# Three of four blocks of turned rows change partition halves by GpSimd's DMA queue instead of narrow TensorE matmuls

## The chip, the cores and the metric

The kernel runs on one core of one Trainium2 chip. The core has TensorE (PE in the profile; PEld is its weight load), VectorE (DVE), ScalarE (ACT), GpSimd (POOL) and SyncE (SP), each with its own instruction queue; they meet at semaphores. DMAs are issued from SP's, ACT's or POOL's queue and are carried by the core's 16 DMA engines. The metric is device time in microseconds, the median of several executions.

## What is computed

The program is a graph network of four layers on N = 3327 nodes with 64 features and one dense adjacency matrix. Each layer is `x = layernorm(x + f(x, adj))`. Layer 0 is cheap here, because its residual needs no product with the adjacency matrix that survives the normalisation in this kernel. The change lies in layer 1, a hyperbolic attention layer, cut to its core:

```python
x_tan = _logmap0(x, C)
left  = x_tan @ att_W[:D] + att_b
right = x_tan @ att_W[D:]
adj_att = jax.nn.sigmoid(left + right.T) * adj
x_local = _logmap(x[:, None, :], x[None, :, :], C)      # for every pair of nodes
support_t = jnp.einsum('ij,ijd->id', adj_att, x_local)
return _proj(_expmap(x, support_t, C), C)
```

For every pair (i, j) a product of two rows gives an angle; the sigmoid of a sum gives an attention weight, which is multiplied by the adjacency entry; and the weighted rows are summed over j. Layers 2 and 3 multiply the adjacency matrix (or counts of its nonzero entries) with the features.

## The kernel before

The nodes are padded to 3328, in 26 blocks of 128. The 64 features take half of the 128 partitions, so two blocks are stacked: a tile of 128 partitions holds block b (0 to 12) in the upper 64 partitions and block b + 13 in the lower 64. The tiles are `ri` and `lj`, rows of i and of j with nodes on partitions, and `riT` and `ljT`, the same turned, with features on partitions.

`near_sphere` (line 1302) is layer 1 for the data at hand. Its main loop runs over `tiles`: for two column ranges of i, for each of the 26 blocks of j, for two chunks of 416 columns. `products` (line 1391) multiplies a block of `ljT` with a chunk of `riT` on TensorE, once in each half of the partitions, into `pq`. `angle` (1406) applies the arc tangent on ScalarE. `attention` (1362) makes the weights: a sigmoid on ScalarE (`sigmoid`) and a product with the adjacency tile on GpSimd (`times`); it is a generator, and its caller decides how far it goes. `gather` (1413) combines angle and weight on VectorE, and `collect` (1436) sums over j on TensorE into `acc`.

A block of j must be multiplied with the i of both halves, so it is needed in both halves of the partitions. `ljT[0]` holds the blocks where the stacking put them, `ljT[1]` holds them with the halves changed. There are two ways to make `ljT[1]`. `wrong` (1487) does it on TensorE: for each block and half a matmul with the identity, 64 columns wide, into the other half of a PSUM tile, which an engine then copies out. `change_over` (1497) does it by two DMAs from `ljT[0]` to `ljT[1]`, one for each half. Before the change, columns of blocks 9 to 12 (with 22 to 25) are made by `wrong` and all others by `change_over` on SP's queue.

The order of the instructions of TensorE, ScalarE, VectorE and GpSimd is written out by hand at lines 1542 to 1657 (`manual_schedule`): each engine's queue follows the order of these lines. `alone` and `bank` (1532 to 1540) take a PSUM tile, run a turn on TensorE at once, and return a function that copies the result out when it is called: on ScalarE by default, on VectorE where `copy` is given. The blocks of j are visited in the order 25, 24, 23, 22, 12, 11, ..., so the first product needs block 12's columns of `ljT[1]`, the third (`products(2)`) block 11's.

The steps around the change, in order: `scaled` and `rows_of_i` on VectorE finish `lj` and `ri`; `after` (1567), a copy of one column by GpSimd, holds that engine's queue until VectorE has finished the last of them; `spread_a` and `spread_b` copy the left terms; `next(start)` runs the first sigmoid and the first `times`; then follow the turns `rows_j` (`right`, blocks 9 to 12), `spread_c`, `spread_d`, `rows_a` (`turn`, blocks 0 to 3), `changed` (`wrong`, blocks 9 to 12) and `rows_b` (`turn`, blocks 4 to 7), each with its copy. A second `next(start)`, the small turns of `prep_few`, the turns of `prep_fours`, and the first products come after these. The blocks of the adjacency matrix are loaded by SP: `kept` (four whole blocks, line 144) and `at` (line 1347).

GpSimd's queue is used for DMAs elsewhere too: at the end of layer 2 it writes and reads back rows of counts (`t_rows`, lines 432 and 464).

Of the kernel before, what the change touches and what calls it, by code (L numbers as in the profile page):

```python
# [23 lines left out]
D = 64  # L24
# [5 lines left out]
def slot(jb):  # L30

    return 2 * (jb % NBH) + jb // NBH
# [50 lines left out]
def kernel(  # L83
# [11 lines left out]
    nc = tc.nc  # L95
# [16 lines left out]
    lj = const.tile([P, NB, D], F32, name="lj")  # L112
# [1077 lines left out]
    with tc.tile_pool(name="l1", bufs=1) as l1:  # L1190
# [18 lines left out]
        with tc.tile_pool(name="l1a", bufs=1) as l1a, tc.tile_pool(  # L1209
# [30 lines left out]
            for i, g in enumerate(range(0, NBH, 4)):  # L1240
                n = min(4, NBH - g)
# [25 lines left out]
            for i, (g, n) in enumerate(turned):  # L1267
                if i == 3:
                    nc.tensor.matmul(n_low, lows, ones, start=True, stop=True)
                for k in range(g, g + n):  # L1270
                    nc.tensor.matmul(
                        pr[:, k].rearrange("p h t -> p (h t)"), xT[:, k * P : (k + 1) * P],
                        attw_c, start=True, stop=True,
# [28 lines left out]
        def near_sphere(mT, ljT_0, xm, sq_e, t_e):  # L1302
# [3 lines left out]
            with tc.tile_pool(name="n1", bufs=1, reuse_waits="tile") as n1, tc.tile_pool(  # L1306
# [10 lines left out]
                ljT = [ljT_0, n1.tile([P, HALF], F32, name="ljT_1")]  # L1317
# [44 lines left out]
                def attention(pair):  # L1362

                    if pair >= len(tiles) // 2:
                        return
                    cp, jb, _ = tiles[2 * pair]
                    at, sl = ats[pair], slot(jb)
                    sg = n1w.tile([P, 2, 2 * CW], F32, tag="sg", bufs=4, name=f"sg_{pair}")
                    lbs = lbh[:, :, cp * 2 * CW : (cp + 1) * 2 * CW]
                    sgs[pair] = sg  # L1370

                    def sigmoid(of):
                        nc.scalar.activation(  # L1373
                            sg[:, :, of], lbs[:, :, of], AF.Sigmoid, bias=rb[:, sl : sl + 1]
                        )

                    def times(h, of):
                        nc.gpsimd.tensor_tensor(  # L1378
                            sg[:, h, of], sg[:, h, of], at[:, h, of], ALU.mult
                        )  # L1380

                    chunks = (slice(0, CW), slice(CW, 2 * CW))
                    sigmoid(slice(0, 2 * CW) if pair else chunks[0])
                    times(slice(0, 2), chunks[0])
                    yield
                    if not pair:
                        sigmoid(chunks[1])
                    times(0, chunks[1])
                    yield
# [104 lines left out]
                            )  # L1494
                    return ljT[1][:, b * P : (b + n) * P], pt[:, : n * P]

                def change_over(b, n):
                    of = slice(b * P, (b + n) * P)
                    nc.sync.dma_start(ljT[1][D:, of], ljT[0][:D, of])
                    nc.sync.dma_start(ljT[1][:D, of], ljT[0][D:, of])  # L1500

                def turn(pt, b, n):

# [7 lines left out]
                def made(pt, make, b, n, at_once=True):  # L1511
                    dst, src = make(pt, b, n)

                    def copy(to=nc.scalar.copy):
                        to(dst, src)
                        if make is right and b < 9:
                            if at_once:
                                change_over(b, n)
                            else:
                                changes.append((b, n))  # L1520

                    return copy
# [9 lines left out]
                def bank(which, make, b, n):  # L1532

                    pt = n1c.tile([P, 4 * P], F32, tag=f"acc{which}", name=f"prep_{make.__name__}_{b}")
                    return made(pt, make, b, n)

                def alone(make, b, n):

                    pt = n1p.tile([P, 4 * P], F32, name=f"first_{make.__name__}_{b}")
                    return made(pt, make, b, n)  # L1540

                with tc.manual_schedule(
# [21 lines left out]
                    scaled(0, 5)  # L1564

                    after = n1.tile([P, 1], F32, name="after")
                    nc.gpsimd.tensor_copy(after, lj[:, 0, :1])
                    spread_a, spread_b = bank(0, left, 0, 4), bank(1, left, 13, 4)
                    spread_a()
                    spread_b()  # L1570
                    for pair in range(4):
                        fetch(pair)
                    start = attention(0)
                    next(start)
                    rows_j = alone(right, 9, 4)
                    spread_c = alone(left, 4, 3)
                    spread_d = alone(left, 17, 3)
                    spread_c()
                    spread_d()
                    rows_j()  # L1580
                    rows_a = alone(turn, 0, 4)
                    rows_a()
                    changed = alone(wrong, 9, 4)
                    changed()
                    rows_b = alone(turn, 4, 4)
                    rows_b(copy)
# [19 lines left out]
                    products(1)  # L1606
                    seventh = bank(0, right, 5, 4)
                    list(attention(1))
                    angle(0)
                    rows_8(copy)  # L1610
                    products(2)
                    for t in range(len(tiles)):
# [5 lines left out]
                        if t % 2 == 0:  # L1618
                            fetch(t // 2 + 4)
                            list(attention(t // 2 + 2))  # L1620
                        if t in (4, 10):
                            change_over(*changes.pop(0))
                        if t == 8:
                            spread_left(7)
                        if t == len(tiles) - 4:
                            of = slice(0, 2 * CW)
# [9 lines left out]
                        if t == len(tiles) - 3:  # L1636
                            pq = n1q.tile([P, 2, 512], F32, tag="pq", name="pq_early")
                            pm = pq[:, :, : 3 * (P + 2)].rearrange("p a (k w) -> p a k w", k=3)
                            for b in range(6):
                                nc.tensor.matmul(  # L1640
                                    pm[:, b // 3, b % 3], mT[:, b * P : (b + 1) * P], all_m,
                                    start=True, stop=True,
# [468 lines left out]
        with tc.If(n_below == 0) as norms:  # L2111
            with ExitStack() as arm:
                with tc.tile_pool(name="n1m", bufs=1) as n1m:
                    mT = n1m.tile([P, HALF], F32, name="mT")
                    ljT_0 = n1m.tile([P, HALF], F32, name="ljT_0")
                    sq_e = n1m.tile([P, 12, D], F32, name="sq_e")
                    t_e = n1m.tile([P, 12], F32, name="t_e")

                    xm = x2.rearrange("p n d -> p (n d)")
                    near_sphere(mT, ljT_0, xm, sq_e, t_e)  # L2120
                    blocks = blocks_ahead(arm)
                    near_end(mT, ljT_0, xm, t_e, x2)
                layers(x2, xc, True, *blocks)
# [43 lines left out]
```

## Time and profile before

| | us |
|---|---|
| median of 3 runs (lowest, highest) | 497.64 (497.33, 497.72) |
| the profiled execution | 499.74 |
| its span, first to last instruction | 498.0 |
| PE busy | 480.5 (96%) |
| DVE busy | 349.2 (70%) |
| ACT busy | 266.3 (53%) |
| POOL busy | 196.8 (40%) |
| mean granted clock of TensorE | 0.981 |

The span is divided so: the first layer and the preparation of layer 1 up to about 26 us, the main loop of layer 1 to about 191, its end to about 211, layer 2 to about 376, and layer 3 with the output after that. Times in the profile are counted from the span's start. In a group or a timeline row the first numbers are start and length, then come engine, line, operation, output tile and input tiles, and in brackets the time for which the engine sat idle before, with what ended it. In the chain of waits each piece is what the following one waited for. The granted clock is a share of TensorE's full speed. A matmul of 32-bit data stands as two records in the profile, a turn (transpose) as one.

### The profile page before, as it was taken

To read this page: it belongs to the slowest core of one execution; us is meant where nothing else is said; L and a number is where in the kernel's file an instruction comes from. 1 tells how busy PE (TensorE), PEld (TensorE's weight loads), DVE (VectorE), ACT (ScalarE), POOL (GpSimd) and SP (SyncE) were. 2 spreads that over 40 slices of the span, in tenths; PEclk is the share of its full clock that TensorE was granted. 3 is DMA by queue.
4 is the path that set the end of the run, shared out by engine and by line. 5 is a ranking of instruction groups with operands and counts; after the bars stand their busy time and mean duration, and the time that the engine had idled before them with its cause. 6 is when DMAs were issued, how large, how long until landed. Compare 5 with 4: busy or idle time off the path is not lost.

```text
span 498.0 us, 7739 instructions
## 1 busy us (share of the span) xinstructions
PE 480.5 (96%) x2865; PEld 220.6 (44%) x2865; DVE 349.2 (70%) x600; ACT 266.3 (53%) x376; POOL 196.8 (40%) x175
## 2 busy tenths in 40 slices
PE   8999999999999999999999999999999999999991
PEld 4733333333333338643434353333345555555551
DVE  6698888878888887995363322656238999689743
ACT  4799999999999985400000000000016876666641
POOL 4299899989999991000000000000352274000000
PEclk9799999999999998999999999999999999999996
DMA  8988988887888278899999009988987699949001
GB/s 273 379 247 281 328 274 273 272 273 259 280 274 276 77 277 314 372 397 428 424 426 384 0 17 403 427 349 334 421 333 235 222 334 387 365 150 356 17 1 42
DMA packets 34186, 139.20 MB, mean 280 GB/s; under 512 B 11231, under 2 KB 13025, under 8 KB 29019
## 3 DMA queue, kind: packets, MB, share of 16 engines
q1 hardware_dynamic: 30603, 137.41, 73.9%
q0 software_dynamic: 1248, 0.64, 0.6%
q10 hardware_dynamic: 2288, 0.57, 0.6%
q8 instruction: 24, 0.39, 0.3%
q14 instruction: 23, 0.19, 0.1%
HBM read 136.93 MB, written 1.04 MB: 277 GB/s over the span
## 4 chain that ended last, share of the span: by engine, by line
PE 80%; DVE 8%; DMA 5%; issue 1%; ACT 1%; SPq 0%; POOL 0%; DVEq 0%
PE cnt L517 26%; PE pq L1400 17%; PE acc L1444 16%; PE cnt L651 5%; PE acc L883 5%; DMA at_l<-in_adjT 3%; PE acc L900 2%; DMA ah<-in_adjT 2%; PE t L452 2%; DVE mask L368 2%; DVE w L667 1%; PE both L752 1%; PE cnt L508 1%; PE pn_l L403 1%; PE pe L1735 1%
## 5 line engine op out<-in xcount | busy, mean ns | idle before, releaser
L1378 POOL TENSOR_TENSOR sg<-sg,at 128x832 f32<-128x832 f32 x88 | 131.2, 1519 | 7.6 <-ACT sg L1373 3.1
L517 PE MATMUL cnt<-at_l,lj 128*64 128x416 f32 x496 | 90.7, 515 | 0.8 <-DMA at_l<-in_adjT 0.8
L1373 ACT ACTIVATE sg<-lb,rb 128x1664 f32<-128x1664 f32 (+1 forms) x53 | 88.0, 1661 | 0.0
L1400 PE MATMUL pq<-riT,ljT 64*128 64x416 f32 x416 | 87.2, 536 | 0.2
L1444 PE MATMUL acc<-v,lj 128*64 128x416 f32 x416 | 85.1, 525 | 0.0
L1409 ACT ACTIVATE pq<-pq 128x832 f32<-128x832 f32 x104 | 83.8, 850 | 1.7 <-issue 1.6
L630 ACT ACTIVATE x<-cnt 128x416 f32<-128x416 f32 x8 | 4.1, 517 | 144.9 <-PE cnt L517 144.9
L669 ACT ACTIVATE w<-cnt 128x416 int16<-128x416 f32 x135 | 63.9, 520 | 28.3 <-PE cnt L651 26.8
L1424 DVE SCALAR_TENSOR_TENSOR v<-pq,sg 128x832 f32<-128x832 f32 x52 | 53.3, 1025 | 18.7 <-ACT pq L1409 18.3
L464 POOL DMA_DIRECT2D t_rows<-tb x4 | 4.1, 1045 | 151.0 <-DVE tb L462 151.0
L1400 PEld LDWEIGHTS pq<-riT,ljT 64*128 64x128 f32 x416 | 35.6, 186 | 49.5 <-ACT pq L1409 30.6
L517 PEld LDWEIGHTS cnt<-at_l,lj 128*64 128x64 f32 x496 | 34.3, 137 | 50.9 <-issue 48.6
L883 PE MATMUL acc<-w,s 128*128 128x416 bf16 x208 | 53.1, 339 | 0.0
L667 DVE TENSOR_SCALAR w<-cnt 128x416 int16<-128x416 f32 x73 | 42.1, 587 | 10.7 <-PE cnt L651 8.3
L1444 PEld LDWEIGHTS acc<-v,lj 128*64 128x64 f32 x416 | 26.0, 136 | 52.2 <-issue 48.4
L517 PE MATMUL cnt<-kept,lj 128*64 128x416 f32 x224 | 41.6, 514 | 0.0
L651 PE MATMUL cnt<-mask,tri 128*128 128x416 bf16 x136 | 35.6, 339 | 2.1 <-DVE w L667 2.1
L368 DVE TENSOR_SCALAR mask<-ah 128x1664 bf16<-128x1664 f32 x34 | 36.4, 1096 | 1.0 <-DMA ah<-in_adjT 1.0
L1421 DVE SCALAR_TENSOR_TENSOR pq<-pq,sg 128x416 f32<-128x416 f32 x52 | 31.2, 600 | 1.8
L445 DVE TENSOR_SCALAR tm<-at_l 128x1664 bf16<-128x1664 f32 x16 | 15.7, 1023 | 22.8 <-PE t L452 20.9
L1420 DVE SCALAR_TENSOR_TENSOR v<-pq,sg 128x416 f32<-128x416 f32 x52 | 30.2, 580 | 0.0
L1044 POOL DMA_DIRECT2D out<-hid x2 | 1.0, 514 | 73.3 <-DVE hid L1049 73.3
(321 smaller groups left out, 525.6 us busy)
## 6 DMA issues: line engine op xcount, KB each, us to landing
at_l<-in_adjT SPq DMA_DIRECT2D x27, 1664.0 KB, 12.3
at<-in_adjT SPq DMA_DIRECT2D x44, 832.0 KB, 5.8
ah<-in_adjT SPq DMA_DIRECT2D x34, 832.0 KB, 6.6
kept<-in_adjT SPq DMA_DIRECT2D x7, 1664.0 KB, 9.6
bt_l<-in_adjT SPq DMA_DIRECT2D x6, 1664.0 KB
lb<-lf_rows SPq DMA_DIRECT2D x2, 384.0 KB
mask<-t_rows SPq DMA_DIRECT2D x34, 3.2 KB
ljT<-ljT SPq DMA_DIRECT2D x4, 128.0 KB
```

Of the source, the lines that this page charges most:

```text
L368: nc.vector.tensor_scalar(mask[q], ahead.pop(q), 0.0, None, ALU.not_equal)
L517: nc.tensor.matmul(acc[c][h * D : (h + 1) * D, :], hw[:, slot(jb), :], blocks[jb][:, o : o + CW], start=c not in begun, stop=last, skip_gr ...
L651: nc.tensor.matmul(cnt[c][e], tri, mask[q][:, of], start=True, stop=True, skip_group_check=True,)
L667: nc.vector.tensor_scalar(to, of, 0.0, None, ALU.max)
L669: nc.scalar.activation(to, of, AF.Relu)
L883: nc.tensor.matmul(acc[h, c][:, e, :], s12[:, slot(jb)].rearrange("p t d -> p (t d)"), ws[q, c, e], start=first, stop=last,)
L1373: nc.scalar.activation(sg[:, :, of], lbs[:, :, of], AF.Sigmoid, bias=rb[:, sl : sl + 1])
L1378: nc.gpsimd.tensor_tensor(sg[:, h, of], sg[:, h, of], at[:, h, of], ALU.mult)
L1400: nc.tensor.matmul(pq[:, h, :], ljT[h != jb // NBH][rows, of], riT[rows, ch * CW : (ch + 1) * CW], start=True, stop=True,)
L1409: nc.scalar.activation(pqs[t], pqs[t], AF.Arctan, bias=ANGLE_FIRST, scale=ANGLE_STEP)
L1424: stt(w, pq, ANGLE_REST, sg, op0=ALU.add, op1=ALU.mult)
L1444: nc.tensor.matmul(accs[cp, ci][h * D : (h + 1) * D, :], lj[:, slot(jb), :], w[:, h, :], start=(jb == orders[cp][0]), stop=(jb == orders[c ...
```

## The change

The turned rows of blocks 9 to 12 are copied out earlier: `rows_j()` moves ahead of `spread_c()` and `spread_d()`. Directly after it, `change_over(9, 3, nc.gpsimd)` issues two DMAs from GpSimd's queue that bring columns of blocks 9, 10 and 11 (with 22 to 24) to the other half of the partitions. Each moves 64 partitions of 384 elements. `wrong` now makes block 12 (with 25) alone. `change_over` gets its queue as an argument. So that the DMAs stand ahead of GpSimd's other work, `after` moves behind them, and `attention` yields once more for pair 0, between its first sigmoid and its first `times`; a further `next(start)` lets that `times` follow `after`.

```diff
                     sigmoid(slice(0, 2 * CW) if pair else chunks[0])
+                    if not pair:
+                        yield
                     times(slice(0, 2), chunks[0])
                     yield
...
-                def change_over(b, n):
+                def change_over(b, n, queue=nc.sync):
                     of = slice(b * P, (b + n) * P)
-                    nc.sync.dma_start(ljT[1][D:, of], ljT[0][:D, of])
-                    nc.sync.dma_start(ljT[1][:D, of], ljT[0][D:, of])
+                    queue.dma_start(ljT[1][D:, of], ljT[0][:D, of])
+                    queue.dma_start(ljT[1][:D, of], ljT[0][D:, of])
...
                     after = n1.tile([P, 1], F32, name="after")
-                    nc.gpsimd.tensor_copy(after, lj[:, 0, :1])
                     spread_a, spread_b = bank(0, left, 0, 4), bank(1, left, 13, 4)
...
                     rows_j = alone(right, 9, 4)
                     spread_c = alone(left, 4, 3)
                     spread_d = alone(left, 17, 3)
+                    rows_j()
+                    change_over(9, 3, nc.gpsimd)
+                    nc.gpsimd.tensor_copy(after, lj[:, 0, :1])
+                    next(start)
                     spread_c()
                     spread_d()
-                    rows_j()
                     rows_a = alone(turn, 0, 4)
                     rows_a()
-                    changed = alone(wrong, 9, 4)
+                    changed = alone(wrong, 12, 1)
                     changed()
```

In the built kernel the order of TensorE's instructions is the same but for the narrow matmuls: two in place of eight. The third product's first matmul waits for the second DMA, in addition to VectorE.

## The prediction

> **What bounds the kernel now.** I read the chain that ended last first. Over the whole span it is TensorE's; from 15 to 32 us, where the change lies, it gives this (start, length, piece):
>
> ```profile
> PE 80%; DVE 8%; DMA 5%; issue 1%; ACT 1%; SPq 0%; POOL 0%; DVEq 0%
> ```
> ```profile
> 16.50 1.11 PE first_right L1481 x4
> 17.61 1.28 PE first_left L1459 x6
> 18.89 0.85 PE first_turn L1505 x4
> 19.75 1.91 PE first_wrong L1491 x16
> 21.65 0.59 PE first_turn L1505 x4
> ...
> 23.00 0.11 issue
> 23.12 0.97 PE pq L1400 x4
> 24.09 0.59 PE prep_fours L1505 x4
> ...
> 25.57 0.59 PE prep_right L1481 x4
> 26.16 1.60 PE pq L1400 x8
> 27.76 2.38 PE acc L1444 x8
> 30.13 1.60 PE pq L1400 x8
> ```
>
> TensorE never rests from 16.50 on, and the narrow turns (first_wrong) stand in that chain, so they are not hidden. Two details matter: four turns cost 0.85 us at 18.89 and 0.59 at 21.65; and the acc group of 27.76 takes 2.38 where later ones take 1.55, a stall of 0.83. From 30.13 to the end of layer 1 near 191 the chain repeats pq 1.60, acc 1.55, all PE, with one break near 112. What start-up saves is therefore carried along.
>
> The first detail is the clock. The table of stretches (PE, its loads, DVE, ACT, POOL, then granted clock, DMA share, GB/s):
>
> ```profile
> 20.00:21.00 1.00, 1.00 (x12) 1.00 (x10) 0.00 (x0) 0.39 (x1) 1.00 (x2) 0.50 0.86 359
> 21.00:22.00 1.00, 1.00 (x12) 0.67 (x9) 0.00 (x0) 0.30 (x1) 1.00 (x1) 0.69 1.03 439
> 22.00:23.00 1.00, 1.00 (x10) 0.75 (x8) 0.69 (x1) 1.00 (x2) 0.02 (x1) 1.00 1.04 429
> ```
>
> The clock is at half from 14.8 to 21.65; all the narrow turns run at half. DMA is full. The second detail is ACT's and DVE's order (timeline of each):
>
> ```profile
> 21.70 0.58 ACT L1515 COPY ljT<-first_wrong 128x512 f32<-128x512 f32 x1 [1.31 <-PE first_wrong L1491]
> 22.18 2.56 ACT L1373 ACTIVATE sg<-lb,rb 128x832 f32<-128x832 f32 x2
> 24.65 1.85 ACT L1409 ACTIVATE pq<-pq 128x832 f32<-128x832 f32 x2
> ```
> ```profile
> 25.60 1.02 DVE L1424 SCALAR_TENSOR_TENSOR v<-pq,sg 128x832 f32<-128x832 f32 x1 [0.20 <-ACT pq L1409]
> 26.54 0.68 DVE L1515 COPY ljT<-prep_right 128x512 f32<-128x512 f32 x1
> 27.34 0.57 DVE L1420 SCALAR_TENSOR_TENSOR v<-pq,sg 128x416 f32<-128x416 f32 x1
> ```
>
> ACT waits 1.31 us for the narrow turns, then runs without a gap; DVE's second tile of products (27.34 to 29.16) is what the long acc group waits for.
>
> **Removed from TensorE.** Eight narrow matmuls (16 records) become two (4): 1.91 x 12/16 = 1.43 us at half clock. The clock's rise I leave at 21.65, since TensorE stays busy. Then the second turn runs at half clock, 0.85 for 0.59, from 20.23 to 21.08; the three prep_few turns cost 0.21 each (0.85/4) for 0.11, to about 21.70. prep_fours (0.44) ends at 22.14 instead of 23.00. DVE's copy of the second turn (0.69) is done at 21.8, so the 0.11 before pq goes: pq 22.16, then 0.97 + 0.59 + 0.90 + 0.59 bring the third pq to 25.2 for 26.16. TensorE's own gain: about 0.95.
>
> **ACT and DVE.** The copy of the narrow turns shrinks to 128 columns (DVE's 128-column copy: 0.28) and follows the riT copy at 20.4; both sigmoids end near 23.1, angles start at 23.2 for 24.65. DVE's first products start at 24.1, its prep_right copy at 25.25 (TensorE ends at 25.2), its second products at 26.05 for 27.34. The long acc group ends 1.3 earlier, its stall shorter. ACT's second angle waits for pq (24.6), a gain of 0.96; ACT starts a pair every 3.09 (26.41 to 29.50) against TensorE's 3.15, and catches up. The sum lies between 0.95 and 1.3; I take 1.1. If the clock's step falls elsewhere in another execution, the removed work is worth 0.7 (12 records at half of 0.119) to 1.43; the runs shown differ by 0.39.
>
> **Moved on ACT.** The rows_j copy (0.59) goes before the two left copies: it starts at 17.65, where ACT idled 0.81; the left copies still end before 19.5, ahead of the turn copy at 19.78. Cost nothing; that idle time covers it.
>
> **Added on POOL.** Two DMAs (64 partitions x 384 elements, 98 KB each) wait for the rows_j copy, so are issued from 18.3. POOL idled 8.57 us up to 19.93 there. The rows nearest in queue and load:
>
> ```profile
> L464 POOL DMA_DIRECT2D t_rows<-tb x4: 630/734/2082, 356.5 to 360.0; - x4
> ```
> ```profile
> DMA to landing us min/median/max: 4.8/5.8/6.6
> ```
> ```profile
> 358.00 1.89 DVE L355 TENSOR_SCALAR kept<-at_l 128x3328 bf16<-128x3328 f32 x1 [1.78 <-DMA at_l<-in_adjT]
> ```
>
> At 0.83 and 0.63 the issues end at 19.8, before POOL's old start: nothing lost. Behind them stand the copy into after and the products of pair 0, wanted by DVE at 24.1 and ready at 22.0 now, so 2 us of cover; at 2.08 per issue POOL is 2.5 late and costs 0.4. Landing: issued at 19.15, second DMA at 24.0 to 25.8, by the median 24.95 (an idle-queue DMA, out<-hid, took 2.1, which gives 21.3). DMA is as full at 356 as here, so I take the median. TensorE's third pq now waits for it and wants it at 25.2; another 0.5 is free, because acc then waits for DVE anyway. So from 25.7 on each us late costs one. What is queued behind that pq: all of TensorE. Traffic of 0.2 MB at 430 GB/s delays block loads by 0.5; they serve products from 28 on and no wait of POOL on a load above 0.2 shows. SP issues the same list as before. The later POOL DMAs take other semaphores of the same ring of eight, still each behind the eighth before; nothing.
>
> The third t_rows DMA (357.93) took the 2.08, and DVE's L355 ran beside it; DVE's instructions from 18.2 to 19.76 are multiplications with two SBUF inputs, of another kind. [...]
>
> The trace shows the clock rising after 18.24 to 21.65, of which turns filled 1.5 us and narrow matmuls 1.9, while 2.5 us of turns between 14.83 and 18.24 with a gap did not raise it (step 3.41, as the dip from 195.7 to 199.1). [...]
>
> **The sum.** Profiled: 499.74, span 498.0; minus 1.1 gives 498.6 and 496.9. The median of the runs, 497.64, is 2.1 below the profiled time; the same 1.1 gives 496.5. One measurement tells about 0.2%, 1.0 us, from no change.
>
> **Rivals.** [...] (2) The DMA lands between 25.7 and 27.0, as the 6.6 counted from a later issue (20.4, after a first issue of 2.08) would: half the gain left, 497.1. [...] (4) The gain is lost later: layer 2 waits 13.94 us for a load at 211.79. But SP issues that load after DVE's end of layer 1, so it moves along. 497.6.
>
> **Chances.** Forecast 0.53, own range 496.1 to 496.9; (1) 0.15; (2) 0.13; (3) 0.13; (4) 0.06. Faster by over 0.2% (below 496.65) is most of the forecast, 0.45; slower is (3) and a tail of (1), 0.15; the rest 0.40. The range goes from 496.0 to 498.2, leaving out (3) and little else.
>
> **What would show it.** Right: first_wrong x4 near 0.5 us; pq's third group at 25.2; no DMA piece in the chain before 30; POOL's products starting near 20.1; the clock rising within the same step. Wrong: a wait of pq on ljT<-ljT, a half clock past 22, or POOL DMA issues over 1 us.

## The result and the profile after

The changed kernel takes 504.89 us in the median (502.19 to 505.75), the kernel before 497.85 (497.33 to 498.44). The ratio on record is 1.0117, with the 95% interval [1.0094, 1.0141], so 1.2% slower; the two medians themselves are 7.0 us apart. I forecast 496.5 and a range up to 498.2. The profiled execution has a span of 503.2 us where that of before, which was 2.1 us over its median, had 498.0.

The place of the loss is plain in the chain that ended last. Shares by engine over the whole span, then its pieces from 18 to 36 us (start, length, piece):

```profile
PE 82%; DVE 7%; DMA 7%; ACT 1%; issue 1%; POOL 0%; SPq 0%; DVEq 0%
```
```profile
18.27 0.48 ACT ljT L1517
18.74 0.30 issue
19.04 0.74 POOL ljT L1501
19.78 0.00 issue
19.79 8.54 DMA ljT<-ljT
28.32 0.14 issue
28.46 3.15 PE pq L1402 x8
31.61 2.82 PE acc L1446 x8
34.42 1.60 PE pq L1402 x8
```

Before, the chain was TensorE's alone here, with the third product at 26.16 (1.60) and the fourth at 30.13. Now a DMA of 8.54 us stands in it, the third product starts at 28.46 and the fourth at 34.42: 4.29 us later. Two things are late. The third product waits, and behind the wait it takes twice its time. GpSimd's timeline, the waits between 14 and 36 us (total, times, longest) and the landing of the two DMAs:

```profile
19.04 0.74 POOL L1501 DMA_DIRECT2D ljT<-ljT  x1 [7.60 <-ACT ljT L1517]
19.79 0.55 POOL L1502 DMA_DIRECT2D ljT<-ljT  x1
20.47 8.83 POOL L1378 TENSOR_TENSOR sg<-sg,kept 128x832 f32<-128x832 f32 x6
```
```profile
ACT pq L1411 <- PE pq L1402: 5.1, 2, 4.6
POOL sg L1378 <- ACT sg L1373: 4.9, 1, 4.9
PE pq L1402 <- DMA ljT<-ljT: 4.7, 1, 4.7
DVE v L1426 <- ACT pq L1411: 4.2, 1, 4.2
```
```profile
DMA to landing us min/median/max: 8.0/8.3/8.5
```

The issues are as quick as forecast. The landing is not: 8.3 us where I had 5.8. TensorE stands for 4.7 us, and ScalarE, VectorE and GpSimd stand behind it for 4 to 5 us each, so nobody works ahead. The table of stretches (PE, its loads, DVE, ACT, POOL, granted clock, DMA share, GB/s) shows the second loss:

```profile
24.00:27.00 3.00, 0.00 (x0) 0.00 (x0) 2.93 (x6) 1.70 (x2) 3.00 (x3) 1.00 0.98 310
27.00:28.00 1.00, 0.00 (x0) 0.00 (x0) 0.03 (x1) 0.00 (x0) 1.00 (x1) 0.66 1.09 295
28.00:29.00 1.00, 0.54 (x2) 0.54 (x4) 0.00 (x0) 0.00 (x0) 1.00 (x2) 0.50 1.08 234
31.00:34.00 3.00, 3.00 (x10) 0.77 (x8) 2.36 (x4) 2.46 (x3) 0.00 (x0) 0.50 1.05 366
```

In the 4.7 us of rest the granted clock falls to a half, at 27.3, and rises again only at 34.1. Of the 4.29 us, 2.30 are the third product's later start (28.46 for 26.16), and 1.99 the longer way from it to the fourth (5.96 for 3.97). From the fourth product on, everything runs 4.29 us behind the profile of before until layer 1's end (the matmuls of `pm` at 195.24 for 190.94). At layer 2's first loads another 0.95 is lost (the products after the load start at 231.01 for 225.77), and this difference, 5.24, stays to the end. The experiments had to explain three things: the late landing, the price of the clock, and that last 0.95.

### The profile page after: what moved, and what is told of

Same layout as the page of the kernel before. It is cut to its first block, busy times and chain, and to the rows that moved or that the text cites. A ratio compares the mean times of both kernels' runs of the same rounds, so it can differ in the third digit from the quotient of the medians.

```text
span 503.2 us, 7721 instructions
## 1 busy us (share of the span) xinstructions
PE 479.1 (95%) x2853; PEld 217.3 (43%) x2853; DVE 349.9 (70%) x600; ACT 265.8 (53%) x376; POOL 198.2 (39%) x177
## 4 chain that ended last, share of the span: by engine, by line
PE 82%; DVE 7%; DMA 7%; ACT 1%; issue 1%; POOL 0%; SPq 0%; DVEq 0%
PE cnt L517 26%; PE pq L1402 16%; PE acc L1446 16%; PE cnt L651 6%; PE acc L883 6%; PE acc L900 3%; DMA at_l<-in_adjT 3%; PE t L452 2%; DMA ljT<-ljT 2%; DVE mask L368 2%; PE both L752 1%; DMA x<-in_x 1%; PE cnt L508 1%; DMA mask<-t_rows 1%; DVE w L667 1%
## 5 line engine op out<-in xcount | busy, mean ns | idle before, releaser
L1402 PE MATMUL pq<-riT,ljT 64*128 64x416 f32 x416 | 88.7, 544 | 4.8 <-DMA ljT<-ljT 4.7
```

Of the source, the lines that this page charges most:

```text
L1402: nc.tensor.matmul(pq[:, h, :], ljT[h != jb // NBH][rows, of], riT[rows, ch * CW : (ch + 1) * CW], start=True, stop=True,)
```

## Experiments

Each is the changed kernel with one edit, compared with the kernel before on the same chip. Where I give us for a ratio, it is the ratio's distance from 1 times 498; the changed kernel itself is then +5.8 (4.7 to 7.0).

### Shorter rows in the loads ahead (e1)

```diff
-keep((NB - 3, NB - 4))
+for jb in (NB - 3, NB - 4):
+    for part in (slice(c * 832, (c + 1) * 832) for c in range(4)):
+        nc.sync.dma_start(kept[jb][:, part], adjT[jb * P : (jb + 1) * P, part])
```

> The changed kernel, but the two adjacency blocks 23 and 22 are loaded in four column quarters each: the same bytes in rows of 3.3 KB instead of 13.3 KB. Theory T1 (the two DMAs of GpSimd's queue wait on the 16 DMA engines behind rows of 13.3 KB that take 0.5 us each; first packet 3.4 us after the issue ended, last engine at 27.6): rows a quarter as long let them in four times as soon, landing 3.5 to 5 us after issue instead of 8.3, TensorE's wait for them below 1 us instead of 4.7, time 497 to 499. Theory T2 (the software queue itself needs that long under load, whatever the other packets' size): landing stays at 8 us, wait 4 to 5 us, time 503 to 506.

Measured: 504.01 us, ratio 1.0088 [1.0055, 1.0121]. Landing and chain:

```profile
DMA to landing us min/median/max: 6.8/7.1/7.4
```
```profile
20.84 7.44 DMA ljT<-ljT
28.41 2.21 PE pq L1402 x8
```

One us less of landing for rows of a quarter of the length, and the DMA still ends at 28.3. That it is the long single rows ahead of a small transfer is refuted as the main cause. Not even the one us is clearly theirs: with eight loads to issue, SyncE issued its `at` load only at 20.38, after the first of the two DMAs, so 832 KB less lay ahead of that one.

### The same DMAs from ScalarE's hardware queue (e2)

```diff
-change_over(9, 3, nc.gpsimd)
+change_over(9, 3, nc.scalar)
```

> The changed kernel, but the same two DMAs are issued from ScalarE's hardware queue, directly after the copy they wait for; ScalarE pays two issues of some 0.5 us. T1 (the engines are full of long rows, whoever issues): landing 7 to 9 us after issue, TensorE waits 3 to 5 us, time 502 to 505. T2 (the cost is the software queue's): landing 3 to 5 us after issue, no or a short wait, time 497 to 498.5.

Measured: 502.14 us, ratio 1.0053 [1.0028, 1.0078].

```profile
DMA to landing us min/median/max: 8.3/8.3/8.3
```
```profile
19.09 8.30 DMA ljT<-ljT
27.52 1.93 PE pq L1402 x8
```
```profile
16.28 1.29 SPq L1347 DMA_DIRECT2D at<-in_adjT  x2
```

The one landing that the view has, the second DMA's, is 8.3 us, as in the changed kernel, though SyncE had issued a second `at` load by then (last line): 4992 KB lay ahead, for 4160. The wait at the third product is shorter, 1.9 for 4.7, because in this execution the issue came 0.7 earlier and TensorE itself was ready 1.9 later. So the late landing does not belong to GpSimd's queue: from ScalarE's, too, it takes 8 us in this place.

### TensorE kept busy while it waits (e3, e8)

```diff
 rows_8(copy)
+for _ in range(40):   # e8: 19
+    nc.tensor.matmul(few[:, 3 * P :], ident, center, start=True, stop=True)
 products(2)
```

> The changed kernel with 40 idle matmuls of 128x128 (about 4.6 us at full clock, results unused) ahead of the third product, where TensorE waits for the DMA. If the fall of TensorE's clock after its wait is a cost of its own (pq x8 3.15 us at half clock instead of 1.60, acc 2.82 instead of 1.6 to 2.4), the clock stays at 1.0 past 28 us and the time falls by about 2 us, to 502.5 to 503.5. If the wait is all of the loss and the slow stretch hides behind ScalarE or VectorE, the time stays at 504 to 506.

Measured: 505.69 us, ratio 1.0141 [1.0116, 1.0167]. The idle matmuls took 8.93 us, twice what I had meant, and themselves held TensorE until 32.85, past the landing at 27.6. The groups behind them were back at 1.60 and 1.55. As built, the run could not tell the price of the clock, so I repeated it with 19.

> The changed kernel with 19 idle matmuls ahead of the third product, 4.2 to 4.5 us by the 0.223 us that each took in the run of forty, from about 23.8 to 28.2, so that TensorE works while it waits and the DMA still ends the wait. If the fallen clock is a cost of its own (pq x8 of 3.15 for 1.60 and acc of 2.82 for 2.38 behind the wait): both at full clock, the third group behind the wait at 32.0 to 32.8 for 34.4, and 1.5 to 2.4 us under the changed kernel. If the lost clock is hidden behind ScalarE's and VectorE's chain, which start up again after the wait too: the same time as the changed kernel, within 0.5.

Measured: 501.53 us, ratio 1.0062 [1.0045, 1.0078], 2.7 us under the changed kernel. The chain, and two stretches of the table:

```profile
24.13 4.24 PE prep_few L1616 x38
28.37 1.64 PE pq L1402 x8
30.01 1.55 PE acc L1446 x8
31.56 1.60 PE pq L1402 x8
```
```profile
24.00:28.00 4.00, 4.00 (x39) 4.00 (x38) 1.20 (x2) 2.03 (x2) 4.00 (x3) 1.00 0.96 317
28.00:32.00 4.00, 4.00 (x24) 1.92 (x24) 3.49 (x7) 2.64 (x3) 1.46 (x2) 1.00 1.04 298
```

The third product starts at 28.37, as late as in the changed kernel, but at full clock. From there to the fourth it takes 3.19 us, not 5.96. So 2.77 us of these two steps are the clock's and not the wait's. (Before, at full clock, they took 3.97, because the acc group stalled; that is why only 1.99 of the loss show there.) The 2.77 us are not hidden behind ScalarE and VectorE, which have to start up again too. The times alone would not show it as well: part of the 2.7 us is layer 2's, where this kernel has one wait and the changed kernel two (below).

### Only two of the three blocks by DMA (e4)

```diff
-change_over(9, 3, nc.gpsimd)
+change_over(9, 2, nc.gpsimd)
...
-changed = alone(wrong, 12, 1)
+changed = alone(wrong, 11, 2)
```

> The changed kernel, but TensorE turns blocks 12 and 11 narrowly (8 records) and the DMAs bring blocks 10 and 9 only, which the fifth product wants, some 3 us after the third. If the landing near 28 us is the whole cause, TensorE wants it at 28 to 29 and waits less than 0.5 us: time 496.8 to 498, the saving of 8 narrow records (0.6 to 0.95 us) less that. If something else in the change costs (the order on ScalarE, GpSimd's start, the added traffic), the time stays above 500.

Measured: 499.30 us, ratio 1.0010 [0.9994, 1.0026]. The landing is nearly as long, but block 11, which the third product reads, no longer comes by DMA; blocks 10 and 9 are wanted later, and no wait on them is in the trace:

```profile
DMA to landing us min/median/max: 6.9/7.5/8.0
```
```profile
25.10 1.67 PE pq L1402 x8
26.77 1.54 PE acc L1446 x6
28.31 0.03 issue
28.34 0.91 PE acc L1446 x2
29.25 1.60 PE pq L1402 x8
```

Nearly the whole slowdown thus hangs on one block, which TensorE wanted 4.7 us before it landed in the changed kernel. What is left, 0.5 us over the kernel before (from 0.3 under to 1.3 over), is not the gain that I had expected of the removed turns. Why it is missing here stays open.

### Loads issued behind the DMAs (e5, e6)

```diff
-keep((NB - 3, NB - 4))
+keep((NB - 3,))                       # e6: neither here
...
 change_over(9, 3, nc.gpsimd)
+nc.gpsimd.dma_start(kept[NB - 4], adjT[(NB - 4) * P : (NB - 3) * P, :])   # e6: NB - 3 ahead of it
```

> The changed kernel, but block 22's load (1.7 MB), which SyncE issued at about 15 us, is issued by GpSimd behind the two DMAs. Theory B (backlog: the two DMAs are served behind what the 16 engines have already been given): ahead of them lie then block 23 and one at load, 2.5 MB from 15 us, which at 0.427 MB a us are through by about 21; the second DMA, issued at 19.8, lands by 22 to 24 (2.5 to 4.5 us from issue, against 8.3), pq does not wait for it, TensorE's clock stays, and the time is 4 to 6 us under that of the changed kernel, between the kernel before and 1 us below it. Theory F (the 8 us belong to this kind of transfer or to its queue, whatever is in flight): landing 7 to 8.5 us, a wait of 4 to 5 us at pq, time 502 to 505.

> As the one before, but block 23's load as well is issued by GpSimd behind the two DMAs, so that nothing but one at load (0.85 MB, through by about 17.5) is ahead of them. Theory B: the second DMA lands 2 to 3 us from its issue, near 22; no wait at pq. But block 23 is issued 5 us later, is there at about 24.5 to 25 and block 22 at 28.5 to 29, and GpSimd's products want them at about 27 and 30: nothing or up to 1 us lost. Time as the run before, to 1 us above it. Theory F: landing 7 to 8.5 us whatever is in flight, time 502 to 505.

Measured: e5 503.98 us, ratio 1.0107 [1.0064, 1.0151]; e6 508.85, ratio 1.0190 [1.0147, 1.0233]. In e5 the landing is 6.6/7.3/8.0 and pq waits 3.9. That looks like the theory of a fixed 8 us, but the edit did not do what it was for. SyncE's timeline of e5:

```profile
14.87 0.34 SPq L144 DMA_DIRECT2D kept<-in_adjT  x1
15.67 2.03 SPq L1347 DMA_DIRECT2D at<-in_adjT  x3
```

With block 22's load gone from its list, SyncE went on at once to three at loads where the changed kernel had issued one. In flight were one load of 1664 KB and three of 832, 4160 KB as in the changed kernel (two and one). In e6 four at loads went ahead, the block that GpSimd issued at 20.57 took 20.5 us to land, and the two DMAs landed after 7.3 and 8.9 us. Both runs only moved the traffic about; they are no test of a free landing, and the next one had to keep SyncE back.

### Almost nothing in flight (e9)

```diff
-keep((NB - 3, NB - 4))
+keep((NB - 3,))
...
 next(start)
+nc.gpsimd.memset(kept[NB - 4][:, :1], 0.0)
+keep((NB - 4,))
...
 at = n1r.tile(...)                    # in load()
+if (cp, jb) == tiles[8][:2]:
+    nc.gpsimd.memset(at[:, 0, :1], 0.0)
 nc.sync.dma_start(at, rows[:, :, of])
```

The fills only tie the two loads to a point in GpSimd's order; the loads write over them.

> The runs with one and with both loads behind did not thin out what is in flight: SyncE went on to its at loads, 2.5 to 3.4 MB, in their place. Here the loads really stay out: block 23's goes as before (through by about 19), block 22's waits for a one-column fill that GpSimd does between the first and the second half of pair 0's products (about 22), and the first at load for one behind pair 1's products (about 26), with all of SyncE's later loads queued behind it. So from 19 to 22 the engines carry the two DMAs alone. Theory B (backlog): the second DMA lands 2 to 3.5 us after its issue, at 22 to 23.5, no wait of pq on it, no fall of the clock behind 24; block 22 is there at 26.5 to 27.5, wanted at about 29, the at loads at 29 to 34, wanted from 34 on; time between the kernel before and 1 us below it, 4 to 7 us under the changed kernel. Theory F (the 8 us belong to this kind of transfer): landing 7 to 8.5, time as the changed kernel or above.

Measured: 499.21 us, ratio 1.0009 [0.9994, 1.0025]. Landing, TensorE's third product, and two stretches of the table while the DMAs are under way (DMA share 0.23 and 0.47, where it is 1.00 in the changed kernel). A wait of 0.5 us is left:

```profile
DMA to landing us min/median/max: 2.3/3.2/4.0
```
```profile
24.61 1.67 PE L1404 MATMUL pq<-riT,ljT 64*128 64x416 f32 x8 [0.51 <-DMA ljT<-ljT]
```
```profile
20.00:21.00 1.00, 0.74 (x6) 0.64 (x6) 0.81 (x2) 1.00 (x4) 1.00 (x3) 1.00 0.23 93
21.00:23.00 2.00, 2.00 (x12) 1.02 (x12) 1.43 (x4) 2.00 (x2) 2.00 (x3) 1.00 0.47 106
```

The same two DMAs from the same queue land in 2.3 to 4.0 us when the engines are free (block 23's load was through at 21.0), against 8.0 to 8.5. The packets say the same: the first one of the two DMAs starts 0.6 us after the first issue's end here, and 3.1 us in the changed kernel. There the DMA queues moved this from 19.79 to 22.95 us (packets, MB, share), q1 for SyncE's loads and q0 for the two DMAs:

```profile
q1 hardware_dynamic: 120, 1.38, 103.7%
q0 software_dynamic: 2, 0.01, 0.7%
```

That SyncE's loads under way cause the late landing is shown. Theory B's law, that the two DMAs wait until the bytes given to the engines before them are through, is not what the runs show. When the first issue ended, 2.84 MB of the loads issued ahead had not been moved in the changed kernel, 4.06 in e2 and 2.31 in e6. The first packet came 3.1, 3.2 and 3.3 us later, and the second DMA landed 8.5, 8.3 and 8.9 us after its issue. At the 426 GB/s of the changed kernel's stretch from 20 to 21 us, e2's 4.06 MB alone would take 9.5 us, but its two DMAs were through at 26.9, 4.4 us ahead of the last of those loads. So a small transfer does not wait for all that was issued before it. Why its first packet needs some 3 us beside loads, no run shows.

But no gain came of it. Of the 5.8 us 5.4 were won back, and the kernel stood where the one before stands.

### What are the removed turns worth? (e7, e10, e11)

e7 and e11 leave the DMAs out and fill the columns with a constant, so that the products of these blocks are of no use. e10 has the new order, all four narrow turns and no DMA.

```diff
-change_over(9, 3, nc.gpsimd)
+nc.gpsimd.memset(ljT[1][:, 9 * P : 12 * P], 0.5)   # e7, e11
```
```diff
-change_over(9, 3, nc.gpsimd)          # e10
...
-changed = alone(wrong, 12, 1)
+changed = alone(wrong, 9, 4)
```

> The changed kernel without the two DMAs: GpSimd fills the other half's columns of blocks 9 to 11 with a constant in their place, early, so that the products of these blocks are of no use, but their work is the same. Left is what the removed narrow turns are worth when nothing has to land. My prediction's sum: 1.1 us under the kernel before (0.7 to 1.4). Rival: the removed turns are worth nothing, because the angles of ScalarE or the products of GpSimd set the pace there; then the time is that of the kernel before, within 0.4. In both cases 5 to 7 us under the changed kernel.

> The changed kernel's order (the copy of blocks 9 to 12 first, GpSimd's small copy behind it, the early products) with all four narrow turns on TensorE again and no DMA. If the order costs nothing, as my prediction had it: the kernel before, within 0.3. If the early copy on ScalarE delays something, up to 0.6 above.

> The kernel without DMAs once more (the columns of blocks 9 to 11 filled with a constant, so these products are of no use), with more rounds and beside the run with the order alone: the first time gave 0.1 us under the kernel before, give or take 0.9, while its own trace ended layer 1 1.75 us earlier than the trace of before, of which two clock steps at half speed in the one and one step in the other are a part. If the removed turns are worth my 0.7 to 1.4: 497.4 to 498.2 where the kernel before has 498.9. If they are worth nothing: within 0.4 of it.

Measured: e7 498.74 us, ratio 0.9998 [0.9980, 1.0017]; e10 498.66, ratio 0.9987 [0.9975, 1.0000]; e11 499.31, ratio 0.9999 [0.9986, 1.0013]. With nothing to land for, the removed turns seemed to be worth nothing. The traces of e10 and of e11 suggest otherwise for layer 1. The narrow turns, first e10, then e11:

```profile
19.91 1.09 PE L1493 MATMUL first_wrong<-ident,lj 128*64 128x128 f32 x16
```
```profile
20.00 0.44 PE L1493 MATMUL first_wrong<-ident,lj 128*64 128x128 f32 x4
```

Sixteen take 1.09 us here and took 1.91 in the profile of before, since the clock had risen already (1.00 from 20 to 22 us in e10, 0.50 from 20 to 21 in before). Counted from the end of the left turns (`prep_left`) to layer 1's `pe` matmuls, layer 1 takes 174.15 us in e10 (17.77 to 191.92) and 173.82 in e11 (17.62 to 191.44): 0.33 are left of the 0.65 that TensorE saves. The same stretch is 173.82 in e7 and 173.81 in e9, but 174.18 in e12 (below), so that single traces do not settle a difference of this size. Then layer 2 takes it back. TensorE's waits for layer 2's loads, first before, then e11:

```profile
222.04 2.96 PE L517 MATMUL cnt<-at_l,lj 128*64 128x416 f32 x16
225.77 3.01 PE L517 MATMUL cnt<-at_l,lj 128*64 128x416 f32 x16 [0.76 <-DMA at_l<-in_adjT]
```
```profile
221.51 3.01 PE L517 MATMUL cnt<-at_l,lj 128*64 128x416 f32 x16 [0.42 <-DMA at_l<-in_adjT]
225.51 3.01 PE L517 MATMUL cnt<-at_l,lj 128*64 128x416 f32 x16 [0.98 <-DMA at_l<-in_adjT]
```

Two waits stand there in the place of one, in the changed kernel, e1, e2, e5, e6, e7, e9 and e11; only one in before, e3, e4, e8 and e10. The first group are just those that issue six matmuls less than before and nothing in their place. What lies there is a 16 KB packet of the instruction queue q8 (24 packets, 0.39 MB in the page of before). The view does not name the engine that it serves; that it is TensorE is my reading, from e12 and e13 below, where six more of TensorE's matmuls move the packet by 7 us. The queue's line for 208 to 212 us of before, and for 213 to 224 us of e11 (packets, MB, share):

```profile
q8 instruction: 1, 0.02, 1.6%
```
```profile
q8 instruction: 1, 0.02, 0.5%
```

In before the packet starts at 210.1 (the expectation of e12 puts it 0.3 later), in a pause of the DMA engines between two loads (their share is 0 in most tenths of a us from 210.4 to 211.8). In e11 it starts at 215.1, among the rows that layer 2 waits for, and takes 0.94 us. In the thirteen traces whose chain has this load, it takes 14.7 to 14.9 us where such a packet falls into it, and 13.5 to 14.1 where none does. Why it takes longer with the packet in it is not shown; no view tells the 16 DMA engines apart.

### The old length of TensorE's instructions (e12, e13)

```diff
-for _ in range(3):
-    nc.tensor.matmul(idle, ident, center_4, start=True, stop=True)
+for w in (2, 2, 2, 1, 1, 1, 1, 1, 1):
+    nc.tensor.matmul(idle[:, : w * P], ident, center_4[:, :w], start=True, stop=True)
```

The idle work at the kernel's very start gets six matmuls more with the same columns in all. e12 is e9 with this edit, e13 is e11 with it.

> The kernel with the loads held back, in which the DMAs land in time, and six matmuls more in TensorE's idle work at the very start: nine of together the same columns instead of three (no change of the result). They give TensorE's instruction stream its old length back. Theory I (instruction fetch): in the profiles of kernels with the twelve records removed and nothing in their place, the 16 KB fetch of TensorE's instructions that lay at 210.4 in the kernel before, between two loads, lies 4 to 5 us later, at 214.7 to 215.4 (220 where layer 1 ends later), inside the loads that layer 2 waits for, takes 0.93 us of one DMA engine there, and layer 2 waits for at_l twice (0.4 to 0.55 and 0.98) in place of once (0.8). With the old length the fetch is back at 209.5 to 211.5, one wait of 0.8 remains, and the time is 0.6 to 0.9 under the 499.2 of the run without the six: 498.3 to 498.6, 0.1 to 0.2% under the kernel before. Rival theory (the second wait comes of the earlier end of layer 1, or by chance): two waits as before, 499.0 to 499.4, the time of the kernel before.

> The same six matmuls in the kernel without DMAs (columns of blocks 9 to 11 filled with a constant, these products of no use), which had 498.7 and 499.3 in its two runs, each with two waits at layer 2. Theory I: one wait of 0.8 at layer 2, fetch at 209.5 to 211.5, 0.6 to 0.9 less, 498.1 to 498.5. Rival theory: two waits, 498.7 to 499.3.

Measured: e12 498.51 us, ratio 0.9989 [0.9972, 1.0007]; e13 497.77, ratio 0.9978 [0.9961, 0.9995]. The packet is back at 208.4 and 208.3, and one wait is left. First e12, then e13:

```profile
224.18 3.01 PE L517 MATMUL cnt<-at_l,lj 128*64 128x416 f32 x16 [0.84 <-DMA at_l<-in_adjT]
```
```profile
223.41 3.01 PE L517 MATMUL cnt<-at_l,lj 128*64 128x416 f32 x16 [0.67 <-DMA at_l<-in_adjT]
```

Nothing but the number of instructions changed from e11 to e13, and from e9 to e12; the ratios fell by 0.0021 and 0.0020, 1.0 us each, and the waits at layer 2 by 0.7 us each (1.40 to 0.67, 1.54 to 0.84). In all fifteen traces two waits and a packet inside the awaited load go together. So the place of the packet is shown to go with the second wait, and six matmuls are shown to move both. That the 1.0 us of time follow from it is likely, but not shown: in each of the two pairs the intervals overlap, and the waits account for 0.7. e12, which leaves nothing out, is the best version of the change; its 0.5 us under the kernel before cannot be told from no change.

## Why the prediction was wrong

**The step that failed: the landing.** I wrote "second DMA at 24.0 to 25.8, by the median 24.95", and "DMA is as full at 356 as here, so I take the median". It landed at 28.3. Of the 3.4 us of difference 0.6 are a later issue (19.79 for 19.15), and 2.7 the landing itself, 8.5 us for 5.8. The runs showed in its place that SyncE's loads make the same two DMAs land after 6.6 to 8.9 us, from either queue, and that without them they need 2.3 to 4.0 (e9), near the 2.1 that I had from an idle queue.

Why the `t_rows` row misled is only partly known. It was near in queue and in the engines' busy time, and near even in the loads still to be moved: 2.6 MB when its first issue began, 3.1 when this one did. Its first packet, too, came 3.1 us after the first issue's end. The difference lies behind the first packet: the first `t_rows` DMA had landed 1.6 us after it, the first `ljT` DMA 4.1 (2.5 in e1). The DMAs there carry 44 KB each and stand among rows of 6.7 KB, these carry 96 and stand among rows of 13.3 KB (3.3 in e1). No run separates the two.

**Rival 3**, the slower one, put the landing at 28.5, within 0.2 us, but counted on a held-up issue and a first issue of 2.08 us. No run shows VectorE holding up GpSimd's issues: they took 0.74 and 0.55 us from 19.04 on, while VectorE was busy for 1.00 of the us from 19 to 20. Its price was wrong too, +1.7 where +5.8 was measured. "From 25.7 each us late costs one" lacked the clock. The wait of 4.7 us made the two steps behind it 2.77 us longer (e8), and in e2 the groups behind a wait of 1.9 were slow too (pq 1.93 for 1.60, acc 2.94 for 1.55).

**The clock.** I asked whether the clock would rise in time (rival 1) and not whether it could fall. In the profile after it had risen at 17.1, against 21.6 before, so rival 1 had no occasion, and TensorE wanted the third product at 23.8, not at 25.2. What decides the rise, no run shows; that it would stay at 21.65 because TensorE stays busy was my estimate. What the profiles of before and after show is lengths: up to 480 us each stretch at half clock is 3.41 or 6.83 us long (6.83 from 14.78 and 3.41 from 195.69 in before, 3.41 from 13.66 and 6.83 from 27.31 in after). The first stretch ends between 17.1 (after) and about 22.0 (e2), from one execution to the next, and the fall in after came 3.6 us into the 4.7 of waiting. In e2, by the lengths of the groups, it came at about 28.8, after a wait of 1.9 us and 1.3 us of work.

**Removed from TensorE.** "1.91 x 12/16 = 1.43 us at half clock" was true of the profiled execution of before, which ran 2.1 us over the median. In thirteen of the fourteen other traces (not in e2) the clock had risen by then; e10 has 0.068 us for a record, not 0.119, so 0.65 (1.09 less e11's 0.44) to 0.82 (12 records) is removed. That was the low end I had kept for "another execution"; the median's distance should have made it the middle.

**The sum, otherwise.** With nothing to land and the instruction packet back in its place, e13 is 1.1 us under the kernel before (0.2 to 1.9), the size I forecast. How much of it is the turns, and how much the order alone (e10: 0.6 under, 0.0 to 1.2), these intervals do not separate. That the size agrees is partly luck: the 1.1 was worked out at half clock, which most executions do not have there.

**Gain lost later (rival 4).** I dismissed it because "SP issues that load after DVE's end of layer 1, so it moves along". It does: 210.67 in e11 for 211.79. But the load then takes 14.79 for 13.94, with something in it that I had not thought of, the packet of instructions.

**Moved on ACT, added on POOL.** Right: the early copy holds up nothing that the traces show, GpSimd's products start at 20.47 (20.1 forecast), and though VectorE waits 0.47 us for the first of them at 23.46, the wait for the landing covers that.

## To carry to other kernels

Price a small transfer beside large loads from a run or a row with transfers of its own size among loads of the same kind. The busy share of the engines (1.0 at both places here) did not tell 5.8 from 8.5 us, and neither did the bytes that were issued ahead. If it is wanted within that time, keep the loads back (2.3 to 4.0 us in e9) or fetch something else by it, as e4 did (499.30 us for 504.89). If TensorE may have to wait 2 us or more for it, add the slow groups behind the wait (0.33 and 1.39 us more after 1.9 us of waiting in e2, 2.77 together after 4.7), or give TensorE idle work there (e8: 1.64 and 1.55). Before an edit of under 1 us is judged, look where the packets of the instruction queue fall among the loads that something waits for; six matmuls fewer moved one by 5 us here (e11: 215.1 for 210.1).

## What the hardware showed

- Two DMAs of 96 KB landed in 8.0 to 8.5 us behind 4160 KB of loads from GpSimd's software queue, in 8.3 us (the second) behind 4992 KB from ScalarE's hardware queue, and in 2.3 to 4.0 us on free engines. In e2 the two DMAs were through 4.4 us ahead of the last of the loads issued before them. But in the eight traces with such loads under way their first packet started only 3.1 to 3.6 us after the first issue's end (0.6 in e9), and in the changed kernel 1.4 MB of the older loads went in that time.
- The later of two 1664 KB loads on GpSimd's queue (block 22 in e6) took 20.5 us to land, behind and beside SyncE's loads.
- The instruction queue q8 moves packets of 16 KB. In the profile of before they come 17 to 29 us apart up to 474 us, closer after that, and take 0.9 to 1.3 us each. Six more of TensorE's matmuls moved one from 215.1 (e11) to 208.3 (e13). No view here names a wait of TensorE for its instructions. But a load that others wait for took 14.7 to 14.9 us with such a packet in it and 13.5 to 14.1 without.
